# Layer 2 attention on one Trainium2 core: merge on 32 partitions, three score buffers, all context keys made early, turns and merges held behind the maxima

## The chip, the cores and the metric

The kernel runs on one core of one Trainium2 chip. The metric is the device time of one execution in microseconds. Before the change three executions took 2648.73, 2651.52 and 2657.36 us; their median is 2651.52 us.

## The reference, cut to what matters

The program is a stack of four layers, each a cross attention followed by a feed-forward part, over x of 4 batches x 256 positions x 256. The change lies in the attention of layer 2. For each batch it has 16 heads of width 128 on 4 key/value heads; the keys are 1601 context rows and then the batch's own 256 rows under a causal mask:

```
q = rope(rms_norm(x @ wq));  k = rope(rms_norm(x @ wk));  v = x @ wv
k_ctx = rms_norm(ctx @ wk_ctx);  v_ctx = ctx @ wv_ctx
k_full, v_full = concat([k_ctx, k]), concat([v_ctx, v])
scores = q . k_full / sqrt(128) + mask      # 256 x 1857 for each head
out = softmax(scores) @ v_full;  return out @ wo
```

## The kernel before, in words

**Units and heads.** `l2_xattn` (L1282) walks over 16 units, one for each batch and key/value head, and in each over 4 query heads: 64 heads. The 1857 keys stand in 15 tiles of 128 (13 of context, where the last is shared with own rows, and own ones).

**Scores.** `scores` (L1488) makes one chunk c of four: 64 of the 256 queries. The stationary operand is 32 queries (128x32), four products lie side by side on the four groups of 32 PSUM partitions (group a takes every tile's keys 32a to 32a+31), so that 448 or 480 key columns stand on 128 partitions as (a, query). A chunk is 8 such products; each is two instructions in the trace. VectorE adds the mask (L1501) and takes the negated maximum (L1504); ScalarE takes the exponential with that bias and sums it up (L1508). Each of the four partition groups so has a maximum and a sum of its own, over a quarter of the keys.

**Merge.** `merge` (L1514) brings the four groups of one head together: TensorE transposes the maxima and the sums (L1519, L1520) to 8 partitions, VectorE takes the least negated maximum, differences, products, sums and reciprocals (L1524 to L1533) with one ScalarE exponential between (L1527), TensorE transposes the shares back (L1535), and VectorE copies them out (L1537). `scale` (L1540) multiplies the exponentials by the shares on GpSimd, eight instructions a head, and `turn` (L1548) transposes 32x32 blocks on VectorE, four instructions a head. `values` (L1554) multiplies by the values: 15 products, in two halves of 8 and 7. `project` (L1565) applies wo once a unit (acc).

**Order.** The loop (L1614 to L1656) writes the order out: for head h it emits two score chunks, the first step of head h-1's merge, the first half of head h-2's values, more of the merge and the scaling of h-1; then two more chunks, the turns of h-1, the second half of the values of h-2. Pieces of the next unit's preparation (`prep`, L1359: q products tpq, own keys and values tpkv, transposes tpqT and tpk, layer norm tp_ln) go between by the tables WHEN, WHEN_EARLY and BETWEEN. The Tile scheduler may then move instructions on an engine by its own estimate; an instruction under `pin` (L99) keeps its place against those traced before and after it. Every engine runs its own list in order.

**Early keys.** The context keys and values of units 0 to 14 (EARLY = 15, L53) are made in `l2_early` (L1202) in pieces that fill idle time of layers 0 and 1, spilled to DRAM (L1236, L1265) and loaded back by `prep`; what is left runs at L1604, before unit 0. Those of unit 15 are made inside `prep` from a second load of the context (ctxT, L1638).

**Banks.** PSUM has 8 banks: two score buffers of two (ps_s), two for all preparation pieces and acc (ps), one for the merge (ps_m), one for values (ps_o).

Of the kernel before, what the change touches and what calls it, by code (L numbers as in the profile page):

```python
# [11 lines left out]
F32 = mybir.dt.float32  # L12
# [5 lines left out]
AF = mybir.ActivationFunctionType  # L18
# [5 lines left out]
P = 128  # L24
B = 4
# [27 lines left out]
EARLY = 15  # L53
# [5 lines left out]
class Kernel:  # L59
# [1222 lines left out]
    def l2_xattn(self):  # L1282
# [11 lines left out]
        with ExitStack() as es:  # L1294
            one = es.enter_context(tc.tile_pool(name="a2one", bufs=1, reuse_waits="tile"))
            two = es.enter_context(tc.tile_pool(name="a2", bufs=2, reuse_waits="tile"))
            ps_s = es.enter_context(tc.tile_pool(name="a2s", bufs=2, space=PSUM))
            ps = es.enter_context(tc.tile_pool(name="a2p", bufs=2, space=PSUM))
            ps_m = es.enter_context(tc.tile_pool(name="a2m", bufs=1, space=PSUM))
# [6 lines left out]
            kw = one.tile([P, 1], F32, name="kw")  # L1306
            nc.scalar.dma_start(kw, i["l2_knw"].rearrange("o p -> p o"))
# [17 lines left out]
            def turned(b):  # L1325

                xn = self.xn.tile([P, 2, D], F32, name="xn")
                self.layernorm(xn, self.x[b])
                if b == 0:
                    self.fill(LN2)  # L1330
                tp = ps.tile([P, 2, 2, P], F32, name="tp_ln", tag="tp")
                for k in range(2):
                    for q in range(2):
                        nc.tensor.transpose(tp[:, k, q, :], xn[:, q, k * P : (k + 1) * P], self.ident)
                t = self.xnT.tile([P, 2, S], F32, name="xT2", tag="xnT")
                nc.scalar.copy(t, tp.rearrange("p k q t -> p k (q t)"))
                return t

            def swapped(ap):
                return ap.rearrange("p h (t d) -> p h t d", t=2)[:, :, ::-1, :]  # L1340
# [4 lines left out]
            def load(g, early):  # L1345
                w = {}
                for n, shape in (("wq", [P, 2, 512]), ("wkc", [P, 2, 256]), ("wks", [P, 2, 256])):
                    if n == "wkc" and early:
                        continue
# [9 lines left out]
            def prep(u, w, ctxT, res):  # L1359
# [3 lines left out]
                early = u < EARLY  # L1363
                va = two.tile([P, NK, HD2], F32, name="va2", bufs=3)
                kT = two.tile([P, NK, P], F32, name="kT2")
                if early:
                    kd, vd = self.early_kv[u]
                    for t, d in ((kT, kd), (va, vd)):
                        nc.sync.dma_start(t[:, :CT, :], d[:, :CT, :])
                    nc.sync.dma_start(kT[:, CT, :96], kd[:, CT, :96])  # L1370
                    nc.sync.dma_start(va[:96, CT, :], vd[:96, CT, :])
# [4 lines left out]
                kr = one.tile([P, NK, HD2], F32, name="kr2")  # L1376
                ss = self.small.tile([P, NK + 8], F32, name="ss2")
                ra, rb = tabs["l2_qnw"]
                qo = []
                for q in range(2):  # L1380
# [6 lines left out]
                    nc.vector.tensor_reduce(ss[:, NK + 4 * q : NK + 4 * q + 4], sq, AX.X, ALU.add)  # L1387
# [11 lines left out]
                def squares(m0, m1):  # L1399
                    n = m1 - m0  # L1400
                    sq = one.tile([P, 4, HD2], F32, name="sq2")
                    nc.scalar.activation(sq[:, :n, :], kr[:, m0:m1, :], AF.Square)
                    nc.vector.tensor_reduce(ss[:, m0:m1], sq[:, :n, :], AX.X, ALU.add)

                if early:
                    nc.gpsimd.memset(kr[:96, CT, :], 0.0)
                for ms in ((12, 13), (14,), (0, 1), (2, 3), (4, 5), (6, 7), (8, 9), (10, 11)):
                    if early and ms[0] < CT:
                        continue
                    tp = ps.tile([P, 2, 256], F32, name="tpkv", tag="tp")  # L1410
                    rows = P
                    for n, m in enumerate(ms):
                        for k in range(2):
                            if m < CT:
                                self.mm(tp[:, n, :], ctxT[:, k, m * P : (m + 1) * P], w["wkc"][:, k, :], k == 0, k == 1)
                            elif m == CT and early:
                                pass
                            elif m == CT:
                                self.mm(tp[:96, n, :], ctxT[:, k, m * P : m * P + 96], w["wkc"][:, k, :], k == 0, k == 1)
# [3 lines left out]
                        if m == CT:  # L1423
                            for k in range(2):
                                self.mm(tp[96:, n, :], xb[:, k, :32], w["wks"][:, k, :], k == 0, k == 1)
                    m, n = ms[0], len(ms)
                    if m == CT and early:
                        for t, v in ((kr, tp[:, :, :HD2]), (va, tp[:, :, HD2:])):
                            nc.scalar.copy(t[96:, CT, :], v[96:, 0, :])
                            nc.scalar.copy(t[:, CT + 1, :], v[:, 1, :])  # L1430
                    else:
                        nc.scalar.copy(kr[:rows, m : m + n, :], tp[:rows, :n, :HD2])
                        nc.scalar.copy(va[:rows, m : m + n, :], tp[:rows, :n, HD2:])
                    if rows < P:
                        nc.gpsimd.memset(kr[rows:, m, :], 0.0)
                    if m == CT + 2:
                        ra, rb = tabs["l2_knw"]
                        ko = one.tile([P, 3, HD2], F32, name="ko2")
                        t2 = one.tile([P, 3, HD2], F32, name="kt2")
                        own = kr[:, CT:, :]  # L1440
                        nc.gpsimd.tensor_tensor(ko, own, ra, ALU.mult)
                        nc.vector.tensor_tensor(halves(t2), swapped(own), halves(rb), ALU.mult)
                        nc.gpsimd.tensor_tensor(ko, ko, t2, ALU.add)
                    if m in (2, 6, 10, 14):
                        squares(CT if m == 14 else m - 2, m + n)
                    yield
                m0 = CT if early else 0
                self.rstd(ss[:, m0:], ss[:, m0:], 1.0 / HD2, self.eps6)
                rq = two.tile([P, 8], F32, name="rq2")
                nc.vector.tensor_scalar(rq, ss[:, NK:], 1.0 / math.sqrt(HD2), None, ALU.mult)  # L1450
# [4 lines left out]
                for m in range(0, 0 if early else CT, 4):  # L1455
                    nc.gpsimd.tensor_tensor(
                        kr[:, m : m + 4, :], kr[:, m : m + 4, :], ss[:, m : m + 4, None].to_broadcast([P, 4, HD2]), ALU.mult
                    )
                for m in range(3):
                    nc.scalar.activation(ko[:, m, :], ko[:, m, :], AF.Copy, scale=ss[:, CT + m : CT + m + 1])  # L1460
# [8 lines left out]
                for m0 in (12,) if early else (0, 4, 8, 12):  # L1469
                    tp = ps.tile([P, 4, P], F32, name="tpk", tag="tp")  # L1470
                    n = min(4, NK - m0)
                    for m in range(n):
                        nc.tensor.transpose(tp[:, m, :], kr[:, m0 + m, :] if m0 < CT else ko[:, m, :], self.ident)
                    if m0 < CT:
                        nc.scalar.activation(kT[:, m0 : m0 + 4, :], tp, AF.Copy, scale=kw)
                    elif early:
                        nc.scalar.copy(kT[:, CT, 96:], tp[:, 0, 96:])
                        nc.scalar.copy(kT[:, CT + 1 :, :], tp[:, 1:n, :])
                    else:
                        nc.scalar.copy(kT[:, m0:, :], tp[:, :n, :])  # L1480
                    yield
# [6 lines left out]
            def scores(kT, qT, h, c, nm, sm):  # L1488
# [15 lines left out]
                nc.vector.tensor_reduce(nm[:, 2 * c : 2 * c + 2], s[:, :, : nt * 32], AX.X, ALU.max, negate=True)  # L1504
                p = main.tile([P, 2, NK * 32], F32, name="p2", bufs=8)
                for n in range(2):
                    e = 2 * c + n
                    nc.scalar.activation(  # L1508
                        p[:, n, : nt * 32], s[:, n, : nt * 32], AF.Exp, bias=nm[:, e : e + 1],
                        accum_out=sm[:, e : e + 1],  # L1510
# [3 lines left out]
            def merge(nm, sm):  # L1514


                t = ps_m.tile([P, 512], F32, name="tm2")
                ct, st = t[:8, 0:P], t[:8, P : 2 * P]
                tc.keep_in_program_order(nc.tensor.transpose(ct, nm, self.ident))  # L1519
                tc.keep_in_program_order(nc.tensor.transpose(st, sm, self.ident))  # L1520
                by = lambda ap: ap.rearrange("n (a j) -> n j a", a=4)
                wide = lambda ap: ap[:, :, None].to_broadcast([8, 32, 4])
                lo = self.small.tile([8, 32], F32, name="lo2")
                nc.vector.tensor_reduce(lo, by(ct), AX.X, ALU.min)  # L1524
                e = self.small.tile([8, P], F32, name="em2", bufs=2)
                nc.vector.tensor_tensor(by(e), wide(lo), by(ct), ALU.subtract)
                nc.scalar.activation(e, e, AF.Exp)  # L1527
                w = self.small.tile([8, P], F32, name="wm2", bufs=2)
                nc.vector.tensor_tensor(w, e, st, ALU.mult)
                tot = self.small.tile([8, 32], F32, name="tot2")  # L1530
# [721 lines left out]
```

## Time and profile before

| | us |
|---|---|
| the profiled execution, its own time | 2653.6 |
| its span, first to last instruction | 2651.9 |
| median of the three executions shown | 2651.52 |
| TensorE busy | 2489.8 (94%) |
| VectorE, ScalarE, GpSimd busy | 1471.6, 1306.1, 746.2 |
| first score product of layer 2's attention | 712.96 |
| its last instruction on TensorE begins (acc) | 1822 |
| mean granted TensorE clock | 0.975 |

The spans of lines are read as follows. A row of the timeline gives the start, the time from the first start to the last end, the engine, the line, the operation and the tiles as output<-inputs, and a count; in square brackets stands the idle time before and what ended it. Matmul ends are modelled and overlap the next start, so TensorE's time is counted here from start to start. L76 is the helper `mm`, so that products are told apart by their tiles: s the scores, o the values, tm the merge.

### The profile page before, as it was taken

The numbers are of one execution on the slowest core, as the hardware profiler recorded it, in microseconds if no ns is written. First come the engines' busy times: TensorE is split into PE (matmuls) and PEld (weight loads), VectorE is DVE, ScalarE is ACT, GpSimd is POOL, SyncE is SP. The second block draws the span as 40 slices with busy tenths as digits, with TensorE's granted clock in tenths as the row PEclk, the third lists the DMA queues.
The fourth block names the chain that finished last, engine by engine and source line by source line (L and its number), as shares of the span: only waits on it lengthen the run. The fifth ranks groups of instructions, "written<-read, shape, count | busy, mean of one in ns | idle before, by whom it ended". The sixth has DMA issues, their size and how long they took to land. (4 is left out here: it accounts for less than half of the span.)

```text
span 2651.9 us, 47069 instructions
## 1 busy us (share of the span) xinstructions
PE 2489.8 (94%) x17800; PEld 1515.1 (57%) x17816; DVE 1471.6 (55%) x3054; ACT 1306.1 (49%) x2973; POOL 746.2 (28%) x1030
## 2 busy tenths in 40 slices
PE   7989986899899999999999999998998999999997
PEld 4678874777545555555555555655564554545553
DVE  6343534753677777777777777774324414233323
ACT  2334443533644445444544444442325775757775
POOL 1014645313334444433443444332102001011000
PEclk8989997999999999999999999998999999999998
DMA  5155574634601111111111110004212100000000
GB/s 201 61 180 151 169 162 150 204 102 153 217 14 46 46 46 46 46 46 46 46 46 46 46 46 21 9 1 155 90 62 66 33 2 27 4 3 2 6 6 5
DMA packets 94656, 186.25 MB, mean 70 GB/s; under 512 B 15053, under 2 KB 62865, under 8 KB 93233
## 3 DMA queue, kind: packets, MB, share of 16 engines
q1 hardware_dynamic: 78278, 144.90, 16.1%
q0 software_dynamic: 10416, 28.46, 4.6%
q10 hardware_dynamic: 5738, 9.87, 1.2%
q8 instruction: 145, 2.38, 0.4%
q14 instruction: 79, 0.64, 0.1%
HBM read 136.77 MB, written 46.42 MB: 69 GB/s over the span
## 5 line engine op out<-in xcount | busy, mean ns | idle before, releaser
L1508 ACT ACTIVATE p<-s,nm 128x448 f32<-128x448 f32 (+1 forms) x512 | 326.5, 644 | 425.1 <-DVE nm L1504 265.1
L1969 ACT ACTIVATE e<-s 128x1024 f32<-128x1024 f32 (+1 forms) x448 | 404.2, 960 | 159.9 <-PE s L76 154.9
L76 PE MATMUL s<-kT,qT 128*32 128x448 f32 (+1 forms) x4096 | 471.9, 558 | 10.0 <-ACT p L1508 5.0
L76 PE MATMUL o<-pT,va 128*128 128x256 f32 (+2 forms) x1920 | 431.0, 376 | 6.0 <-DVE pT L1550 6.0
L1544 POOL TENSOR_SCALAR p<-p,rm 128x448 f32<-128x448 f32 (+1 forms) x512 | 322.5, 652 | 370.9 <-DVE rm L1537 340.6
L76 PEld LDWEIGHTS o<-pT,va 128*128 128x128 f32 (+1 forms) x1920 | 344.4, 191 | 92.9 <-issue 51.4
L1550 DVE STREAM_TRANSPOSE pT<-p 128x896 f32<-128x896 f32 (+1 forms) x256 | 283.8, 1127 | 36.6 <-POOL p L1544 33.0
L1504 DVE TENSOR_REDUCE nm<-s 128x2 f32<-128x896 f32 (+1 forms) x256 | 282.7, 1104 | 3.3
L76 PE MATMUL s<-qb,kT 32*128 32x256 f32 (+1 forms) x3328 | 267.1, 404 | 13.2 <-ACT e L1969 11.0
L76 PEld LDWEIGHTS s<-kT,qT 128*32 128x32 f32 x4096 | 124.0, 110 | 266.3 <-issue 225.2
L76 PE MATMUL o<-e,va 128*32 128x256 f32 (+1 forms) x3328 | 236.1, 392 | 1.3 <-DVE os L2066 1.3
L76 PEld LDWEIGHTS s<-qb,kT 32*128 32x128 f32 (+1 forms) x3328 | 162.6, 181 | 105.8 <-issue 76.2
L76 PEld LDWEIGHTS o<-e,va 128*32 128x32 f32 (+1 forms) x3328 | 90.6, 110 | 115.0 <-issue 74.9
L1996 POOL TENSOR_TENSOR x<-x,t 128x32 f32<-128x32 f32 x64 | 14.7, 250 | 438.6 <-DVE t L1991 438.6
L76 PE MATMUL fill<-wkc_early,ctxT 128*128 128x256 f32 (+1 forms) x532 | 129.2, 393 | 2.8 <-ACT kT_early L1264 2.4
L1501 DVE TENSOR_TENSOR s<-s,mask 128x128 f32<-128x128 f32 (+1 forms) x256 | 83.1, 325 | 69.3 <-PE s L76 64.1
L76 PEld LDWEIGHTS fill<-wkc_early,ctxT 128*128 128x128 f32 (+1 forms) x532 | 103.2, 196 | 20.8 <-ACT kT_early L1264 4.2
L433 POOL DMA_INDIRECT f0xr<-f0xd,f0src x95 | 91.1, 959 | 63.6 <-PE f0gu L76 18.1
L1396 POOL TENSOR_TENSOR qo<-qo,qt 128x512 f32<-128x512 f32 x32 | 41.0, 1283 | 226.0 <-DVE rm L1537 139.6
L1508 ACT ACTIVATION_READ_ACCUMULATOR p<-s,nm 128x1 f32 x512 | 101.7, 199 | 0.0
L76 PE MATMUL f2gu<-f2wgu,f2xsT 128*128 x176 | 84.1, 601 | 0.6 <-ACT f2xsT L73 0.3
L76 PE MATMUL filly<-wkc_early,ctxT 128*128 128x256 f32 (+1 forms) x248 | 67.1, 417 | 13.7 <-ACT kT_early L1264 11.9
(517 smaller groups left out, 3584.1 us busy)
## 6 DMA issues: line engine op xcount, KB each, us to landing
ctxT<-in_ctxT SPq DMA_DIRECT2D x10, 1664.0 KB
f0yd<-f0ys SPq DMA_DIRECT2D x95, 128.0 KB
vd<-va_early SPq DMA_DIRECT2D x90, 128.0 KB
kd<-kT_early SPq DMA_DIRECT2D x45, 256.0 KB
kT<-kd SPq DMA_DIRECT2D x15, 768.0 KB
va<-vd SPq DMA_DIRECT2D x15, 768.0 KB
wq<-in_l_wq SPq DMA_DIRECT2D x16, 512.0 KB
wo<-in_l_wo SPq DMA_DIRECT2D x16, 512.0 KB
```

Source lines behind the costliest of these rows:

```text
L76: self.nc.tensor.matmul(out, lhsT, rhs, start=start, stop=stop, **kw)
L433: nc.gpsimd.indirect_dma_start(out=t, out_offset=None, in_=xd[:, :], in_offset=bass.IndirectOffsetOnAxis(ap=src[:, n : n + 1], axis=0),)
L1396: nc.gpsimd.tensor_tensor(o1, o1, t2, ALU.add)
L1501: nc.vector.tensor_tensor(sv, sv, mask[:, 2 * c : 2 * c + 2, : nt - CT, :].rearrange("p n t i -> p n (t i)"), ALU.add)
L1504: nc.vector.tensor_reduce(nm[:, 2 * c : 2 * c + 2], s[:, :, : nt * 32], AX.X, ALU.max, negate=True)
L1508: nc.scalar.activation(p[:, n, : nt * 32], s[:, n, : nt * 32], AF.Exp, bias=nm[:, e : e + 1], accum_out=sm[:, e : e + 1],)
L1544: nc.gpsimd.tensor_scalar(p[:, n, : nt * 32], p[:, n, : nt * 32], r[:, e : e + 1], 1.0, ALU.mult, ALU.mult)
L1550: nc.vector.transpose(pT[:, 2 * c : 2 * c + 2, :nt, :].rearrange("p n t i -> p n (t i)"), p[:, :, : nt * 32])
L1969: nc.scalar.activation(e[:kr, :, :n, :], s[t][:kr, :, :n, :], AF.Exp, scale=1.0 / math.sqrt(HD3))
L1996: nc.gpsimd.tensor_tensor(xt, xt, t[:, q], ALU.add)
```

## The change

- `EARLY` becomes 16: unit 15's context keys and values join `l2_early`. `prep` loses its late branch, `load` loses wkc, the loop loses the load of ctxT, and `kr` and `ss` shrink to the 3 own tiles.
- PSUM: three score buffers (6 banks), one bank for ps, none for the merge.
- `merge` works on 32 partitions: GpSimd copies the four partition groups' maxima and sums side by side (4 instructions of 32x16), VectorE works on 32x32 elements, GpSimd multiplies the shares back out to the four groups (4 instructions of 32x8). No TensorE instruction is left in it.
- The merge's first reduction and the turns are pinned, so VectorE keeps them behind the maxima that the loop emits ahead of them. In the built program VectorE's list for a head reads: mask, maximum, mask, maximum, the five merge operations, mask, maximum, mask, maximum, four turns; TensorE's reads: two chunks, 8 values, two chunks, 7 values, with whole preparation pieces between.
- After each square root of layer norm and key norm a one-column exponential is issued on ScalarE (`exps_next`), pinned.
- One table WHEN takes the place of two.

```
-EARLY = 15
+EARLY = B * NKV2
...
-            ps_s = es.enter_context(tc.tile_pool(name="a2s", bufs=2, space=PSUM))
-            ps = es.enter_context(tc.tile_pool(name="a2p", bufs=2, space=PSUM))
-            ps_m = es.enter_context(tc.tile_pool(name="a2m", bufs=1, space=PSUM))
+            ps_s = es.enter_context(tc.tile_pool(name="a2s", bufs=3, space=PSUM))
+            ps = es.enter_context(tc.tile_pool(name="a2p", bufs=1, space=PSUM))
...
+            def exps_next():
+                self.pin(nc.scalar.activation(self.small.tile([P, 1], F32, name="one2"), self.eps6, AF.Exp))
...
+            def merge(ms):
+                c = self.small.tile([32, 4, 2, 8], F32, name="ms2")
+                for a in range(4):
+                    nc.gpsimd.tensor_copy(c[:, a], ms[32 * a : 32 * a + 32])
+                by = lambda ap: ap.rearrange("j a n -> j n a")
+                wide = lambda ap: ap[:, None, :].to_broadcast([32, 4, 8])
+                lo = self.small.tile([32, 8], F32, name="lo2")
+                self.pin(nc.vector.tensor_reduce(lo, by(c[:, :, 0]), AX.X, ALU.min))
+                e = self.small.tile([32, 4, 8], F32, name="em2")
+                nc.vector.tensor_tensor(e, wide(lo), c[:, :, 0], ALU.subtract)
+                nc.scalar.activation(e, e, AF.Exp)
+                yield
+                w = self.small.tile([32, 4, 8], F32, name="wm2")
+                nc.vector.tensor_tensor(w, e, c[:, :, 1], ALU.mult)
+                tot = self.small.tile([32, 8], F32, name="tot2")
+                nc.vector.tensor_reduce(tot, by(w), AX.X, ALU.add)
+                nc.vector.reciprocal(tot, tot)
+                r = self.small.tile([P, 8], F32, name="rm2")
+                for a in range(4):
+                    nc.gpsimd.tensor_tensor(r[32 * a : 32 * a + 32], e[:, a], tot, ALU.mult)
                 return r
...
             def turn(p, pT, c):
                 nt = tiles_of(c)
-                nc.vector.transpose(
+                self.pin(nc.vector.transpose(
                     pT[:, 2 * c : 2 * c + 2, :nt, :].rearrange("p n t i -> p n (t i)"), p[:, :, : nt * 32]
-                )
+                ))
...
-            WHEN = [2, 2, 2, 3, 2, 0, 2, 2]
-            WHEN_EARLY = [0, 1, 1, 2, 1, 0, 2, 1]
-            BETWEEN = [0, 0, 0, 0, 0, 0, 1, 1]
+            WHEN = [0, 1, 1, 1, 2, 0, 1, 1]
+            BETWEEN = [0, 0, 0, 0, 0, 0, 0, 1]
...
-                            if not early and (b1 != b or ctx is None):
-                                ctx = self.load_ctxT(one, b1, 1)
-                            w = load(g1, early)
-                            pieces = prep(n + 1, w, ctx, ready)
+                            w = load(g1)
+                            pieces = prep(n + 1, w, ready)
```

## The prediction

> **What bounds the kernel now.** I read first the busy time by stage: ahead of layer 2's attention, in 13 of its middle units, and in its last unit with the tail.
>
> ```profile
> core 0: us, PE busy (x) PEld busy (x) DVE busy (x) ACT busy (x) POOL busy (x), PEclk, DMA share, GB/s
> 640.00:709.00 69.00, 58.72 (x272) 46.00 (x271) 37.91 (x93) 37.55 (x103) 27.22 (x33) 0.95 0.72 235
> 770.00:1655.00 885.00, 879.00 (x5653) 486.21 (x5651) 677.47 (x1145) 421.78 (x1191) 353.90 (x515) 1.00 0.13 43
> 1736.00:1823.00 87.00, 80.63 (x491) 48.82 (x489) 55.97 (x91) 27.76 (x82) 25.68 (x43) 0.98 0.00 1
> ```
>
> In the long middle of layer 2 (13 units, 770 to 1655) TensorE is busy 879 of 885 us at granted clock 1.00; VectorE has 77%, ScalarE 48%, GpSimd 40%. Then what TensorE waits for there:
>
> ```profile
> engine line waited for: us in total, times, longest us
> PE s L76 <- ACT kT L1478: 4.0, 3, 1.3
> PE tm L1535 <- DVE em L1533: 1.2, 3, 0.4
> ```
>
> 5.2 us in 885: buffers and maxima cost TensorE nothing there, and a gain must come out of its own list. That list, from its timeline (start, length, tile):
>
> ```profile
> 1146.64 0.59 PE L76 MATMUL tpkv<-wks,xT 128*96 128x256 f32 x2
> 1147.16 3.21 PE L76 MATMUL s<-kT,qT 128*32 128x448 f32 x32
> 1150.31 0.27 PE L1519 MATMUL tm<-ident,nm 128*8 128x128 f32 x1
> 1150.41 0.27 PE L1520 MATMUL tm<-ident,sm 128*8 128x128 f32 x1
> 1150.52 3.36 PE L76 MATMUL o<-pT,va 128*128 128x256 f32 x16
> 1153.81 3.43 PE L76 MATMUL s<-kT,qT 128*32 128x480 f32 x32
> 1157.17 1.13 PE L76 MATMUL o<-pT,va 128*128 128x256 f32 x4
> 1158.23 0.22 PE L1535 MATMUL tm<-ident,em 8*128 8x8 f32 x1
> 1158.39 2.42 PE L76 MATMUL o<-pT,va 128*128 128x256 f32 x10
> ...
> 1171.72 0.99 PE L76 MATMUL s<-kT,qT 128*32 128x480 f32 x2
> 1172.64 0.22 PE L1535 MATMUL tm<-ident,em 8*128 8x8 f32 x1
> 1172.80 3.42 PE L76 MATMUL s<-kT,qT 128*32 128x480 f32 x30
> 1176.15 3.29 PE L76 MATMUL o<-pT,va 128*128 128x256 f32 x14
> 1179.28 0.49 PE L1473 MATMUL tpk<-ident,ko 128*128 128x128 f32 x3
> 1179.60 0.60 PE L1334 MATMUL tp_ln<-ident,xn 128*128 128x128 f32 x4
> 1181.55 0.96 PE L76 MATMUL s<-kT,qT 128*32 128x448 f32 x8 [1.34 <-ACT kT L1478]
> ```
>
> Two score chunks take 3.36 us where nothing is between (1153.81 to 1157.17), and 4.43 us where the one small transpose em falls into a group of four side-by-side products (1171.72 to 1176.15): it breaks the group in two. That happens in three of the four heads of each of these units.
>
> **The change, part by part.** Starts to starts, on TensorE, for a unit in the middle:
>
> - em gone: 3 x (4.43 - 3.36) = 3.21. In the fourth head it stands among values: 1157.17 to 1160.65 is 3.48, the same seven without it (1176.15 to 1179.28) 3.13: 0.35.
> - The transposes of maxima and sums gone: 1150.31 to 1150.52 is 0.21, and going straight from scores to values costs 0.02 more than going to the transpose: 4 x 0.19 = 0.76.
> - One tpq stands split, half of it between two score chunks (1059.97 to 1064.31, 4.34 with 3.15 of scores; other half 0.95): 2.14 together. A whole one behind values takes 1.81 (1195.75 to 1197.56). The built order has it whole: 0.33 less. tpkv and tpqT, together now, are split in two by the new order; each further change between narrow and full products costs about 0.1: 0.2 more.
> - tpk now stands directly ahead of the next unit's scores, which need the two kT copies on ScalarE. Before, a tpq covers them in most units, leaving a 0.13 us wait. ScalarE must first copy the last values out (it ended at 1179.85 in this unit), then the kT copies (1181.03 to 1181.49, 0.46 us), then 0.05 to the product: about 1180.37, 0.77 us after TensorE has nothing else. 0.64 more. Bounds: 0 if the scheduler's order hides it, 1.95 as between 1179.60 and 1181.55, where the exponentials stood ahead.
>
> Sum 3.21 + 0.35 + 0.76 + 0.33 - 0.2 - 0.64 = 3.81 us a unit. From tpk to tpk 13 units take 888.85 us (769.77 to 1658.62). Of these, 3 have the 1.34 us idle shown above, where the new wait takes the place of a longer one: 3.6 more. **-13 x 3.81 - 3.6 = -53.1.**
>
> **Unit 15's keys.** 26 products (two instructions of 0.216, 0.432 each) and 13 transposes of 0.109 are 12.65 us. They leave unit 14's interval, 77.70 us against 67.99 the one ahead; as a plain unit it would take 68.0 - 3.8 = 64.2: **-13.5**. They go ahead of unit 0, where TensorE already waits 4.3 us (2.3 for qo from GpSimd, the rest for copies, 688 to 709), which they cover. But the last keys' normalization stands uncovered: copies, square root with a table load (1.28), GpSimd's four products (L1253, 1.04) against 0.44 of transposes each; only 13 transposes and a tpq stand between. I put 4.5 us, near the 5.0 us wait for va_early (L1235) at 660 to 665. **+12.65 - 4.3 + 4.5 = +12.9**, bounds +8 and +18. Transfers: 11 spills (1.7 MB) are added to SP's queue, and the ctxT load (1664 KB) and wkc (256 KB) leave it; those stood in this same stretch (DMA share 0.72), so its load stays. The four reloads fall into unit 14, at a share of 0.02.
>
> **Unit 0.** Its products wait 5.0 us for exponentials (two buffers, an Exp table load of 1.28) and 1.7 for turns; its merges cost about 2.3. With three buffers the chunks run on, and the first values wait for the first head's turns; I leave 2.5. **-6.5** (-3 to -10).
>
> **Last unit and tail.** 1736.32 to the last chunk's end is 59.1 us: three split groups, four pairs of transposes and one em among values, 4.4, and 1.5 of waits go; without preparation pieces about 1.5 of new waits come, and 0.3 for kT: **-4.1**. The tail's chain (exponentials, merge, eight scalings of 0.63, turns, values) loses two passes through TensorE and gains eight small GpSimd instructions: **-1** (-3 to +3).
>
> **What must hide.** The turns on VectorE now come behind the fourth maximum, and the next head's first values need all four. From the fourth chunk's end E: mask 0.33, maximum 1.10 and 0.1 of signalling, then four turns, 4.5 us (1.127 each) to 4.96 (as at 1160.51, beside GpSimd): E + 6.1 to 6.5. TensorE meanwhile has 7 values 3.13, a piece (tpq 1.81; tpkv 2.04; acc 3.55; transposes and the kT wait 1.6), two chunks 3.18: E + 7.9 at the least. 1.4 us to spare. Behind a late turn on VectorE stand the q products and the next masks and maxima, for which ScalarE's exponentials wait; three score buffers hold that off for a chunk more.
> The scalings must be ahead of the turns. From the previous head's E': the turns end at 6.3, two maxima 9.2, reduction and difference 9.7, ScalarE behind four exponentials (0.64 each) 10.9, three VectorE operations 11.7, four GpSimd products 12.5, eight scalings 17.6. The last turn wants to start at 19.4 or later. So the chain has 1.8 us here and 1.4 above, 3.2 in all. In the third head GpSimd's ko (1.38 + 1.0) falls between the scalings, but acc (3.55) is behind them.
> The small operations are not in this trace. GpSimd: between 0.11 (a memset, L959) and 1.27 (128x512, L1396); the nearest is 128x32 at 0.25 (L1996): I take 0.2. GpSimd's load rises by 1.6 us a head to some 8.5 of 16. VectorE's merge falls from 2.15 us (seven rows) to about 1 (reciprocal of 128x11: 0.19; bounds 0.7 and 1.8). The pinned reduction waits for GpSimd's copies, done at about E' + 5.6, long ahead of 9.2. One bank for ps: its pieces stand at least 3 us apart, their copies take 0.6 to 2. exps_next moves table loads, of which there are as many.
>
> **Sum.** -53.1 - 13.5 + 12.9 - 6.5 - 4.1 - 1 = -65.3. The profiled execution took 2653.6 us (span 2651.9; 2.1 above the median of 2651.52): **2588 us**. With the bounds of the terms (kT wait 0 or 1.95: -12, +18; the keys ±5; unit 0 ±3.5) 2570 to 2612.
>
> **A rule against it.** The Trainium skill, TensorEngine Tiling (Array Packing), section Instruction Overhead, has a matmul cost about 60 cycles however few columns it has. By it a removed transpose is worth only its own short issue. The rows say 1.07 us where it splits a group, and they decide; what only the issue would give is the third rival.
>
> **Rivals.**
> - *The turns come late.* The 1.4 us of cover is lost in part (turns slowed by GpSimd, q products of 2 us on VectorE ahead of the masks). For: VectorE at 77% with a fixed order. Against: the spare time above. At 0.5 us a head, 64 heads: +32, 2620. **0.16.**
> - *GpSimd becomes the bound (slower).* No row shows GpSimd moving data from one group of partitions to another. Per head it has 8 scalings 5.1, its other work 1.85, and eight small ones: from 1.27 us each this fills the 17.1 us that a head takes now, and the chain's 3.2 us are used up too. At 1.98 (L1727, its longest plain row) a head takes 22.8: 64 x 5.7 = +365, 3018. Against: all small rows lie at 0.1 to 0.3. **0.06.** The Trainium skill (GPSIMD Engine Reference, Engine selection) has two-input elementwise work about twice as slow there as on VectorE; twice the 0.366 of L1533 would stay under that point.
> - *Only the issue is saved.* The groups stay as slow for another reason: 0.37 x 64 = 24, less 10 for kT, and 5 at both ends: 2634. Against: the plain 3.36 stands in each unit. **0.04.**
> - Gains and new waits cancel: **0.04.**
>
> **How the numbers follow.** The forecast has 0.70. The range 2565 to 2630 holds nearly all of it and most of the late turns. Faster by over 0.3% (8 us, about what a measurement of this kernel can tell from none): 0.70 + 0.16 + 0.04 = 0.90; same 0.04; slower 0.06.
>
> **What would show it.** Two chunks at 3.2 and 3.4 us in all heads and none at 4.4; tpk to tpk near 64 us; TensorE's waits in the middle only for kT, about 0.8 a unit; the stretch from the last layer-1 product to the first score 13 us longer; no waits for pT. Wrong would be waits of o for pT in every head, GpSimd's small rows over 0.5 us, or the stretch ahead of unit 0 over 20 us longer.

## The result, and the profile after

The changed kernel takes 2581.26 us (median of five, 2579.31 to 2583.5) against 2650.18 for the kernel before (median of five, 2648.73 to 2657.36) on the same chip: ratio **0.9736, 95% interval 0.9723 to 0.9749** (time divided by that of the kernel before, so below 1 is faster). The forecast was 2588, in a range of 2565 to 2630. The profiled execution has a span of 2581.7 us, 70.2 less than before.

Busy time by stage, the same three stages of the changed kernel; the columns are those of the rows before:

```profile
642.00:711.00 69.00, 61.76 (x286) 48.88 (x285) 37.82 (x91) 43.13 (x114) 27.19 (x32) 0.98 0.69 221
775.00:1608.00 833.00, 825.85 (x5511) 475.95 (x5509) 636.65 (x1045) 423.90 (x1210) 434.68 (x937) 1.00 0.14 47
1672.00:1750.00 78.00, 73.57 (x475) 46.51 (x473) 51.77 (x81) 25.97 (x80) 32.75 (x80) 1.00 0.00 1
```

The 13 middle units take 833 us where they took 885, and TensorE is still busy in nearly all of it (825.85): its list became shorter, not its waits. Its only wait there, 0.55 us in each unit:

```profile
engine line waited for: us in total, times, longest us
PE s L76 <- ACT kT L1446: 7.1, 13, 0.6
```

TensorE's list in the middle, from the changed kernel's timeline:

```profile
1145.73 3.21 PE L76 MATMUL s<-kT,qT 128*32 128x448 f32 x32
1148.88 3.46 PE L76 MATMUL o<-pT,va 128*128 128x256 f32 x16
1152.17 0.60 PE L1439 MATMUL tpqT<-ident,qo 128*128 128x128 f32 x4
1152.70 3.43 PE L76 MATMUL s<-kT,qT 128*32 128x480 f32 x32
1156.06 0.65 PE L1439 MATMUL tpqT<-ident,qo 128*128 128x128 f32 x4
1156.55 3.19 PE L76 MATMUL o<-pT,va 128*128 128x256 f32 x14
1159.58 0.49 PE L1444 MATMUL tpk<-ident,ko 128*128 128x128 f32 x3
1160.62 3.21 PE L76 MATMUL s<-kT,qT 128*32 128x448 f32 x32 [0.55 <-ACT kT L1446]
```

Both pairs of chunks run whole in 3.15 to 3.36 us, start to start; no tm product is left. VectorE around the same head:

```profile
1154.59 0.37 DVE L1467 TENSOR_TENSOR s<-s,mask 128x192 f32<-128x192 f32 x1 [1.85 <-PE s L76]
1154.99 1.16 DVE L1470 TENSOR_REDUCE nmsm<-s 128x2 f32<-128x960 f32 x1
1156.20 0.37 DVE L1467 TENSOR_TENSOR s<-s,mask 128x192 f32<-128x192 f32 x1
1156.60 1.16 DVE L1470 TENSOR_REDUCE nmsm<-s 128x2 f32<-128x960 f32 x1
1157.67 4.21 DVE L1515 STREAM_TRANSPOSE pT<-p 128x896 f32<-128x896 f32 x4
1162.39 0.30 DVE L1467 TENSOR_TENSOR s<-s,mask 128x128 f32<-128x128 f32 x1 [0.51 <-PE s L76]
```

Masks and maxima wait for nothing but their scores, and the four turns run behind them without a gap. They end at 1161.88; the values that need them start at 1163.76, 1.9 us later. The costliest rows of the page give the merge's new GpSimd products beside the scalings:

```profile
L1509 POOL TENSOR_SCALAR p<-p,rm 128x448 f32<-128x448 f32 (+1 forms) x512 | 324.4, 655 | 6.2
L1502 POOL TENSOR_TENSOR rm<-em,tot 32x8 f32<-32x8 f32 x256 | 54.5, 213 | 399.3 <-DVE tot L1499 388.0
```

By stage, from the two profiled executions:

| us | before | after | difference | forecast |
|---|---|---|---|---|
| start to the last product of layer 1 | 646.2 | 644.0 | -2.2 | 0 |
| from there to unit 1's tpk (keys ahead, unit 0) | 123.6 | 131.0 | +7.4 | +6.4 |
| 13 middle units | 888.8 | 833.5 | -55.4 | -53.1 |
| unit 14 | 77.7 | 64.0 | -13.7 | -13.5 |
| last unit | 59.2 | 53.8 | -5.4 | -4.1 |
| tail of layer 2's attention | 26.9 | 24.0 | -2.9 | -1 |
| all behind it | 829.5 | 831.4 | +1.9 | 0 |

### The profile page after: what moved, and what is told of

It is laid out like the page before. It is cut to its first block, busy times and chain, and to the rows that moved or that the text cites. A ratio compares the mean times of both kernels' runs of the same rounds, so it can differ in the third digit from the quotient of the medians.

```text
span 2581.7 us, 47099 instructions
## 1 busy us (share of the span) xinstructions
PE 2429.5 (94%) x17609; PEld 1503.7 (58%) x17625; DVE 1415.9 (55%) x2928; ACT 1313.5 (51%) x3005; POOL 842.5 (33%) x1545
## 5 line engine op out<-in xcount | busy, mean ns | idle before, releaser
L1474 ACT ACTIVATE p<-s,nmsm 128x448 f32<-128x448 f32 (+1 forms) x512 | 326.5, 644 | 379.5 <-PE s L76 244.3
L76 PE MATMUL s<-kT,qT 128*32 128x448 f32 (+1 forms) x4096 | 425.1, 556 | 8.6 <-ACT kT L1446 8.2
L1470 DVE TENSOR_REDUCE nmsm<-s 128x2 f32<-128x896 f32 (+1 forms) x256 | 287.5, 1124 | 8.0
L1515 DVE STREAM_TRANSPOSE pT<-p 128x896 f32<-128x896 f32 (+1 forms) x256 | 270.7, 1112 | 9.4 <-POOL p L1509 8.8
L1502 POOL TENSOR_TENSOR rm<-em,tot 32x8 f32<-32x8 f32 x256 | 54.5, 213 | 399.3 <-DVE tot L1499 388.0
L76 PE MATMUL fill<-wkc_early,ctxT 128*128 128x256 f32 (+1 forms) x584 | 143.7, 396 | 6.7 <-ACT kT_early L1264 5.5
L76 PEld LDWEIGHTS fill<-wkc_early,ctxT 128*128 128x128 f32 (+1 forms) x584 | 112.5, 196 | 27.8 <-ACT kT_early L1264 8.3
L1474 ACT ACTIVATION_READ_ACCUMULATOR p<-s,nmsm 128x1 f32 x512 | 101.5, 198 | 0.0
```

Source lines behind the costliest of these rows:

```text
L76: self.nc.tensor.matmul(out, lhsT, rhs, start=start, stop=stop, **kw)
L1470: nc.vector.tensor_reduce(ms[:, 0, 2 * c : 2 * c + 2], s[:, :, : nt * 32], AX.X, ALU.max, negate=True)
L1474: nc.scalar.activation(p[:, n, : nt * 32], s[:, n, : nt * 32], AF.Exp, bias=ms[:, 0, e : e + 1], accum_out=ms[:, 1, e : e + 1],)
L1502: nc.gpsimd.tensor_tensor(r[32 * a : 32 * a + 32], e[:, a], tot, ALU.mult)
L1515: self.pin(nc.vector.transpose(pT[:, 2 * c : 2 * c + 2, :nt, :].rearrange("p n t i -> p n (t i)"), p[:, :, : nt * 32]))
```

## The experiments

Of the twelve kernels, e1 to e4 and e9 to e12 ran on two other chips, on both of which the kernel before takes about 2615 us; in these runs the last product of layer 1 stands near 610 us in place of 645. Therefore only ratios to the kernel before on the same chip, and the mean time of the 13 middle units (68.37 us before, 64.11 after), are compared.

**What a small product costs inside a group.** e5 puts one product as small as em into a group of four side-by-side score products, once a head; e6 puts the same product between two groups. In both the score products are pinned, and the product writes to columns that nothing reads.

```
+  if c == 2 and (n, a) == (1, 0):      # e6: (0, 3)
+      self.pin(nc.tensor.matmul(s[:, 1, 504:512], self.ident[:8, :], self.ident[:8, :8], start=True, stop=True))
```

> The changed kernel with one added product a head, as small as em (8 rows, 8 columns, into unused columns of the score buffer, read by nobody), after the fifth of eight products of the third chunk, so inside a group of four; score products pinned. Theory: 1.07 us a head, 64 x 1.07 = 68: about 2650. Rival (only the issue): 0.15 a head, 10 us: about 2591.

> The same added product, but after the fourth of the eight, between two groups. Theory: its own 0.15 and a change of shape of 0.11, 64 x 0.26 = 17: about 2598, some 50 us less than inside a group. Rival (only the issue): the same as inside the group, 2591.

The unit is 69.03 us in e5 (ratio 1.0041, 1.0027 to 1.0054) and 65.92 in e6 (0.9857, 0.9837 to 0.9876). First e5's timeline, then e6's:

```profile
999.55 1.80 PE L1461 MATMUL s<-kT,qT 128*32 128x480 f32 x10
1001.27 0.38 PE L1466 MATMUL s<-ident 8*128 8x8 f32 x2
1001.59 2.62 PE L1461 MATMUL s<-kT,qT 128*32 128x480 f32 x22
1004.13 2.21 PE L76 MATMUL o<-pT,va 128*128 128x256 f32 x9
```

```profile
999.84 1.01 PE L1461 MATMUL s<-kT,qT 128*32 128x480 f32 x8
1000.78 0.38 PE L1466 MATMUL s<-ident 8*128 8x8 f32 x2
1001.09 2.62 PE L1461 MATMUL s<-kT,qT 128*32 128x480 f32 x24
1003.65 3.29 PE L76 MATMUL o<-pT,va 128*128 128x256 f32 x14
```

The two chunks take 4.58 us with the product inside a group and 3.81 at its edge, where an undisturbed pair takes 3.36. The place alone costs (69.03 - 65.92) / 4 = **0.78 us** a head, against 0.81 expected. The rival that only the issue is saved falls. At the edge the product costs 0.45, more than the 0.26 expected, and inside 1.23, more than the 1.07 of em: it is two instructions (0.31 us from start to start), where em is one (0.15). The difference between e5 and e6 is free of that, since both hold the same product.

**The same cure in the kernel before.** e1 pins the score products and em, so that em splits no group:

```
-  self.mm(
+  self.pin(nc.tensor.matmul(
...
-  nc.tensor.transpose(t[:, 256:264], e, self.ident[:8, :8])
+  self.pin(nc.tensor.transpose(t[:, 256:264], e, self.ident[:8, :8]))
```

> The kernel before, with the score products and the back transpose em pinned, so that em stands between values or at a chunk's edge and splits no group of four score products; all three transposes of the merge stay. Theory (the gain lies on TensorE's own list, mostly in split groups): em costs about 0.26 us outside a group and 1.07 inside, three times a unit, so 2.4 us a unit, some 39 us in all, less about 10 for single values that now stand between score chunks: near 2622 us. Rival (only the issue of the transposes is saved): no transpose is saved here, so the kernel before, 2650 within 5. Rival (buffers and VectorE's order carry the change): neither is touched, also 2650.

Measured 1.0041 (1.0026 to 1.0056), a unit of 67.86. TensorE's busy time in the middle fell from 879 to 860 us, but its waits rose from 5 to some 19 (for at, kT, pT and p, about equal), and single products of values, tpq and acc stood between score chunks. The expectation missed; the time is nearer to the rivals' forecast, and slower still. The 13 middle units did gain 6.7 us; unit 0 lost 7.7 (64.5 us from the first score product to unit 1's tpk, against 56.8) and the last unit 3.6. By itself e1 doesn't tell the price of a split, since the pins changed the order of everything; e5 and e6 do.

**The pins away.** e4 is the changed kernel without its two pins:

```
-  self.pin(nc.vector.tensor_reduce(lo, by(c[:, :, 0]), AX.X, ALU.min))
+  nc.vector.tensor_reduce(lo, by(c[:, :, 0]), AX.X, ALU.min)
...
-  self.pin(nc.vector.transpose(
+  nc.vector.transpose(
```

> The changed kernel without the pins on the turns and on the merge's first reduction; VectorE's list is then the scheduler's. Theory: VectorE has 1.9 us to spare at the turns, so the order costs little either way: 2581 within 8. Rival (the held order carries the change): 20 us or more slower than the changed kernel.

Measured 1.0023 (1.0010 to 1.0037), a unit of 69.02: the whole gain is gone, with all else of the change in place. The expectation missed, and the rival held. Waits of TensorE in e4's middle units:

```profile
PE s L76 <- ACT p L1474: 20.1, 13, 1.7
PE tpqT L1439 <- ACT qT L1440: 13.1, 13, 1.0
PE s L76 <- ACT kT L1446: 8.1, 10, 3.0
PE tpk L1444 <- ACT qT L1440: 7.0, 3, 2.3
```

**The merge alone.** e7 is the kernel before with the new merge and ps_m dropped: two score buffers, EARLY = 15, the old tables, no pins.

> The kernel before with the new merge alone (32 partitions, GpSimd's copies and products, no transposes on TensorE); two score buffers, unit 15's keys late, no pins on VectorE, old tables. Theory: all that TensorE's list gains is here: about 4 us a unit, 16 units, and none of the costs ahead of unit 0: 2588 within 8. Rival (buffers and VectorE's order carry it): 2625 or more. Rival (only the issue): 24 us, 2626.

Measured **1.0259** (1.0239 to 1.0280), a unit of 73.53: the shorter list by itself made the kernel slower. My theory, that the list carries the gain, fell here. VectorE's list in e7 shows why:

```profile
1269.39 2.34 DVE L1548 STREAM_TRANSPOSE pT<-p 128x896 f32<-128x896 f32 x2 [2.50 <-POOL p L1542]
1271.66 0.65 DVE L1569 TENSOR_TENSOR x<-x,acc 128x512 f32<-128x512 f32 x1
1272.23 1.16 DVE L1548 STREAM_TRANSPOSE pT<-p 128x960 f32<-128x960 f32 x1
1273.31 0.27 DVE L1500 TENSOR_TENSOR s<-s,mask 128x128 f32<-128x128 f32 x1
1273.49 1.16 DVE L1548 STREAM_TRANSPOSE pT<-p 128x960 f32<-128x960 f32 x1
1274.57 1.05 DVE L1503 TENSOR_REDUCE nmsm<-s 128x2 f32<-128x896 f32 x1
```

The first turn waits 2.50 us for GpSimd's scaling. Behind it stand the mask and the maximum of a chunk that TensorE had finished near 1268.5 (its pair started at 1266.90): its maximum starts at 1274.57. Then ScalarE's exponentials are late, both score buffers stay full, and TensorE stops. Its own row, and e7's waits in the middle units:

```profile
1277.13 3.43 PE L76 MATMUL s<-kT,qT 128*32 128x480 f32 x32 [2.76 <-ACT p L1507]
```

```profile
PE s L76 <- ACT p L1507: 85.6, 42, 4.0
```

**List and order together.** The new theory: the list is a gain where VectorE's order is held. e9 is e7 with both pins.

> The kernel before with the new merge and both pins; two score buffers, two banks for preparation, unit 15's keys late and the old tables stay. Theory (the short TensorE list and VectorE's held order are both needed and together enough): a middle unit near 64.3 us (64.1 as after the change, about 0.2 for products of tpq that stand split), TensorE's waits there under 1 us a unit, no waits for exponentials; ratio to the kernel before 0.973 to 0.980. Rival (buffers, tables or early keys are a third condition): a unit over 66 us with waits for p as in the kernel with the merge alone, ratio 0.99 or more.

Measured **0.9726** (0.9709 to 0.9744), a unit of 63.59. e9's middle row:

```profile
733.00:1558.00 825.00, 824.66 (x5503) 474.27 (x5502) 629.62 (x1044) 418.67 (x1192) 431.85 (x934) 1.00 0.14 46
```

TensorE is busy 824.66 of 825 us. Buffers, tables and early keys are no third condition, and `exps_next`, which e9 lacks as well, is none either: e9 is as fast as the changed kernel (0.9736), by their intervals. Its unit 14, which holds the last keys, takes 75.9 us against 64.0, but its way from layer 1 to unit 1's tpk only 119.3 against 131.0. The two pins are the only difference from e7: 9.9 us a unit.

**Which pin.** e10 is the changed kernel with only the turns pinned, e11 with only the reduction pinned; each diff is one half of e4's.

> The changed kernel with only the turns pinned; the merge's reduction and difference then stand ahead of the next two masks and maxima in VectorE's list, and one product of the merge ahead of the first maximum. Theory (the turns, which wait for GpSimd's scalings, are what holds the maxima up; the reduction waits for copies that are done by then): a unit 64 to 65 us, ratio 0.974 to 0.985. Rival (either pin alone is not enough, since the merge's product waits for a ScalarE exponential): a unit of 66.5 us or more with waits for p, ratio 0.99 or more.

> The changed kernel with only the merge's reduction pinned; the turns stand among the next head's masks and maxima, the second one ahead of the first maximum. Theory (the turns' place decides): close to the kernel with no pin, a unit 67 to 69 us with waits of s for p and kT, ratio 0.99 to 1.003. Rival (the reduction's place decides): a unit of 64 to 65 us, ratio 0.974 to 0.985.

e10: 0.9727 (0.9708 to 0.9746), a unit of 64.11, as after the change. e11: 0.9997 (0.9984 to 1.0010), a unit of 68.76. The turns' pin carries all of it. VectorE in e11, at the end of a unit:

```profile
1137.87 1.11 DVE L1515 STREAM_TRANSPOSE pT<-p 128x896 f32<-128x896 f32 x1 [2.48 <-POOL p L1509]
1138.90 0.33 DVE L1467 TENSOR_TENSOR s<-s,mask 128x192 f32<-128x192 f32 x1
1139.15 1.09 DVE L1515 STREAM_TRANSPOSE pT<-p 128x896 f32<-128x896 f32 x1
1140.16 1.12 DVE L1470 TENSOR_REDUCE nmsm<-s 128x2 f32<-128x960 f32 x1
1141.20 0.35 DVE L1467 TENSOR_TENSOR s<-s,mask 128x192 f32<-128x192 f32 x1
1141.47 1.16 DVE L1515 STREAM_TRANSPOSE pT<-p 128x960 f32<-128x960 f32 x1
1142.55 1.12 DVE L1470 TENSOR_REDUCE nmsm<-s 128x2 f32<-128x960 f32 x1
```

The maxima stand between turns again; the last one ends at 1143.67. Behind it come ScalarE's last two exponentials and its copy of the values (at, 1145.05), and TensorE waits for that copy:

```profile
1142.22 0.49 PE L1444 MATMUL tpk<-ident,ko 128*128 128x128 f32 x3
1145.47 1.17 PE L76 MATMUL o<-pT,va 128*128 128x256 f32 x2 [2.76 <-ACT at L1528]
1146.57 4.38 PE L76 MATMUL s<-kT,qT 128*32 128x448 f32 x32
```

The waits rose by 35 us over the 13 units (42.5 against 7.1), expected for p and kT, measured mostly for at (27.8). TensorE's busy time rose by 24.6 (850.46 against 825.85), of which the last row shows a piece: a pair of chunks at 4.31 us, start to start, in place of 3.15 (the clock, see the last section).

**Two score buffers.** e2 is the changed kernel with `bufs=2` for ps_s and `bufs=2` for ps.

> The changed kernel with two score buffers again, and two banks for the preparation pieces. Theory: TensorE waited for no score buffer in the middle units before, so a unit stays at 64 us; only unit 0 loses 2 to 3 us. 2584 within 6. Rival (buffers carry it): most of the 70 us come back, above 2610.

Measured 0.9715 (0.9702 to 0.9727), a unit of 63.54, no wait of TensorE in the middle. The third buffer isn't needed. With two preparation banks the scheduler put half a tpq behind tpk, or the layer norm's transposes in three of the 13 units, which covers the kT copies.

**tpk a step earlier.** e3 is the changed kernel with other tables and the score products pinned:

```
-  WHEN = [0, 1, 1, 1, 2, 0, 1, 1]
-  BETWEEN = [0, 0, 0, 0, 0, 0, 0, 1]
+  WHEN = [0, 1, 1, 1, 2, 0, 1, 0]
+  BETWEEN = [0, 0, 0, 0, 0, 0, 1, 1]
```

> The changed kernel with WHEN and BETWEEN set so that tpk stands ahead of the last seven values of a unit, and the score products pinned. Theory: the wait for the kT copies (0.55 us a unit) goes, and nothing takes its place: 15 x 0.55, about 8 us less than the changed kernel, 2573. Rival: tpqT comes earlier and waits for GpSimd's last work on q, which gives the time back: 2581 or more.

Measured 0.9715 (0.9699 to 0.9732), a unit of 63.49, no wait: the kT wait is the order's, not the bank's alone.

**Early keys alone.** e8 is the kernel before with EARLY = 16.

> The kernel before with EARLY = 16 and nothing else. Theory: unit 14 gives back 10 us (77.7 to 68), the stretch ahead of unit 0 takes 13: 2653 within 6. Rival (making the keys early is a gain by itself): 2642 or less.

Measured 1.0018 (1.0007 to 1.0029): the keys' products move from unit 14 to the stretch ahead of unit 0 (140.6 us to unit 1's tpk, against 123.6) and gain nothing; by the interval the kernel is a little slower.

**The best version.** e12 is e2 and e3 together.

> The changed kernel with two score buffers, two banks for preparation, tpk one step ahead and the score products pinned: the two versions that had no wait for kT, put together. Theory (what is left in a unit is TensorE's list, 63.5 us, whichever way the kT wait is covered): a unit 63.4 to 63.6 us, no waits of TensorE in the middle, ratio 0.970 to 0.973, so no gain over either alone. Rival (with two buffers and tpk ahead the waits for p come back, since nothing covers a late maximum): a unit over 64.5 us, ratio over 0.976.

Measured **0.9697** (0.9681 to 0.9713), a unit of 63.45, no wait in the middle. It beats the changed kernel's 0.9736 (intervals apart), as 13 x 0.66 = 8.6 us of units would have it. Against e2 or e3 alone the intervals overlap.

## Why the prediction was right

- **The bound.** Right: TensorE's list bounds the middle before and after, and e9 and e12 show the same with no wait left.
- **em out of the groups (3.21 a unit).** Right: the place costs 0.78 a head by e5 and e6, where 0.81 was expected from the rows (1.07 inside, 0.26 outside). The Trainium skill, TensorEngine Tiling (Array Packing), Key Properties, has a change of the tiling mode drain TensorE. That fits a product between groups that still costs 0.45; the page gives no price.
- **The unit (64.2).** Measured 64.11. The terms can be told apart by summing each tile's time from start to start over the 13 units of both traces. Scores, values and the merge's transposes together fell by 4.54 us a unit (scores 28.98 to 26.01, transposes 1.49 to 0, values 25.84 to 25.76), where the terms 3.21, 0.35 and 0.76 make 4.32; this is mainly where the 13 units gained more than forecast (2.3 us in all). tpq fell by 0.27 (0.33 forecast), and tpkv and tpqT together rose by 0.14 (0.2 forecast). tpk with the kT wait behind it rose by 0.71, where 0.77 was worked out for that wait. The profile's 0.55 for it counts from tpk's modelled end and is another length.
- **The keys and unit 0.** Their sum was +6.4 and came to +7.4, partly by luck. The first score product came 13.4 us later after layer 1 (80.2 against 66.8), and the stretch from there to unit 1's tpk took 6.0 less (50.8 against 56.8), where +12.9 and -6.5 were forecast. But one tpq of 1.9 us moved from behind the first scores to ahead of them; without it the terms are +11.5 and -4.1, both off, in opposite directions. The wait for the last keys' normalization was 2.5 us (for kr_early), where 4.5 was put. The first values of unit 0 waited 2.2 us for turns, where 2.5 was left, and the second head's values another 3.4 that no term held. That nothing is gained by moving the keys is confirmed by e8. The -13.5 of unit 14 and the +12.9 ahead were rightly seen as one move.
- **Last unit and tail.** Both gave more than the forecast, 1.3 and 1.9 us; none of the runs took these apart. The -2.2 and +1.9 us of the first and last stage stand outside the change and cancel by chance.
- **What must hide.** Right in size: 1.9 us to spare ahead of the values, where 1.4 at the least was worked out; small GpSimd operations of 0.19 to 0.21, where 0.2 was taken; five VectorE rows of 0.18 to 0.20 for the merge, where 1 us was taken. So the rivals of late turns and of GpSimd as the bound did not come about, outside unit 0.
- **What the prediction left unpriced.** It put the gain down to the list and saw in the held order only a risk. The runs show it as a condition: with the order free the same list is worth 1.0023 (e4) or 1.0259 (e7). The sentence "behind a late turn on VectorE stand ... the next masks and maxima" named the place, but it named it for the changed kernel, where the order prevents it. A forecast for the merge alone by the same sum was 2588 and would have been wrong by 135 us.
- **What stays open.** The kernel before holds no turn either, and in three of four heads its turns stand among the maxima, as here:

```profile
1174.94 1.10 DVE L1550 STREAM_TRANSPOSE pT<-p 128x896 f32<-128x896 f32 x1
1175.97 1.12 DVE L1504 TENSOR_REDUCE nm<-s 128x2 f32<-128x960 f32 x1
```

So in that kernel the place alone does little harm; in e7 and e11 a turn in that place waits far longer for its scaling. VectorE's waits for scalings ahead of turns in the 13 middle units of the kernel before, of e7 and of e11:

```profile
DVE pT L1550 <- POOL p L1544: 25.9, 39, 1.4
DVE pT L1548 <- POOL p L1542: 126.5, 72, 2.8
DVE pT L1515 <- POOL p L1509: 122.5, 65, 2.5
```

In e4 they are 100.0 us; where the turns are held (the changed kernel, e9, e10) there are none. Why the turns of the new merge wait so much longer for their scalings than those of the old one was not tried. Nor was the old merge with its turns held; TensorE waits there for 5.2 us of 885, so VectorE's order had little to give back.

## What to carry to other kernels

On an engine with a strict list, an instruction that waits for a slow engine should stand behind those that release the bounding engine; here a shorter list on the bound was a gain only where that order was held, so price the order as well as the list. A small product inside a group of side-by-side products costs far more than its own row (1.23 us against 0.38 here): look for it in the pace of its neighbours, and move it off TensorE or to the edge of a group (0.45).

## What the runs showed of the hardware

**The split of a group.** A product of 8 columns costs 1.23 us a head inside a group of four 32-column products ((69.03 - 64.11) / 4) and 0.45 at its edge, though its own two instructions span 0.38 us. em, one instruction of 0.22, cost 1.07 inside a group.

**Half pace after a wait.** After a wait of TensorE of some length, its products run for about 3 to 7 us at half pace: in e11 a row of four side-by-side score instructions of 448 columns takes 0.75 us from start to start in place of 0.38. The granted clock (the share of TensorE's full clock that the profile records) is 0.50 in that very stretch, and the pace is whole again when it is back at 1.00. e11 behind the wait that ends at 1145.47, with the columns of the rows by stage:

```profile
1145.60:1149.00 3.40, 3.40 (x18) 1.10 (x22) 0.00 (x0) 0.18 (x1) 0.41 (x3) 0.50 0.00 0
1149.00:1156.00 7.00, 7.00 (x62) 3.93 (x56) 3.63 (x9) 3.37 (x10) 0.83 (x5) 1.00 0.00 0
```

In the middle units of e4, e7 and e11 this followed all 16 waits of over 3.3 us and none of the 42 between 0.9 and 2.0; between 2.0 and 3.1 us it followed in 12 of 18. So such waits cost more than they show: in e11 35 us more of waits came with 25 us more of busy time, and its 13 units hold 51 us at clock 0.50 (a mean of 0.97 in 893 us), which at half pace is 25.6 us lost. The Trainium skill, TensorE: Matmul & The Clock Gate, HAM oscillation, puts the limit at gaps above about 3.4 us. Here the three waits of 2.3 us of tpk for qT in e4 sufficed.

**Small GpSimd operations.** Copies of 32x16 from one group of partitions to another take 0.19 us (187 to 193 ns), products of 32x8 0.21, so moving four groups side by side and back costs 1.6 us a head.
